# A two-layer decoder on one core: self-attention units in three pieces instead of four, later transposes, and a normalization moved to GpSimd

## The chip, the cores and the metric

The kernel runs on one core of a Trainium2 chip. The core has five engines with queues of their own: TensorE (PE; its weight loads are listed apart as PEld), VectorE (DVE), ScalarE (ACT), GpSimd (POOL) and SyncE (SP), which only issues DMAs here. Each engine takes its instructions in the order of the program and waits on semaphores. Matmul results go to PSUM, which has 8 banks of 128 x 512 float32. The metric is the device time of one execution in microseconds (us); less is better.

## The reference, cut to what matters

Two post-norm decoder layers over x (4 batches, 512 positions, 256 features), all in float32. The last layer is what the change touches:

```python
def _L1_attn_ref(x, w_qkv, w_out):           # 16 heads of 16, causal
    q, k, v = split(x @ w_qkv.T)
    scores = q @ k.T / 4 + (1 - tril) * -10000.0
    return (softmax(scores) @ v) @ w_out.T
def _L1_xattn_ref(x, ctx, ctx, mask, ...):    # 16 heads, 1601 keys
    Q, K = rope(x @ Wq.T + bq), rope(ctx @ Wk.T + bk)
    return softmax(where(mask, Q @ K.T / 4, -inf)) @ V @ Wo.T + bo
...
x = _layernorm(x + _L1_attn_ref(x, ...))
x = _layernorm(x + _L1_xattn_ref(x, ctx_1024, ctx_1024, mask, ...))
x = _layernorm(x + _L1_ffn_ref(x, ...))       # starts with a layernorm of its own
```

Before it stand the first layer's attention-like recurrence, a cross-attention and a mixture of experts, which take the first 920 us or so and are not changed.

## The kernel before, in words

The function `last_layer` (line 1278) holds the whole last layer. Its body is emitted under a manual schedule: each engine runs its instructions in the order in which the Python code emits them, and nothing is reordered. It is built twice, for `causal` true and false, and a value computed on the chip picks one; in the profile the true one ran (the affine selects of line 1599 and the score matmuls of 128, 256, 384 and 512 columns exist only there).

**Units.** The work is cut in 32 units (line 1312): first 16 of self-attention (4 batches by 4 groups of 4 heads), then 16 of cross-attention. A unit has steps, one for each key tile of 128 keys: 4 in self-attention, 13 in cross-attention. The loop over them starts after `for i, u in enumerate(units)`. A step emits:

- `scores` (1579): for each of the 4 heads a matmul of keys by queries into a bank of its own. A head uses 32 of the 128 rows of the array. In self-attention key tile k is seen only by queries from 128 k on, so the columns are 512, 384, 256 and 128.
- between the two halves (2 heads each) two calls of `next1` -> `slot1` (1509): matmuls of a *later* unit's scores, transposed, into a bank for each of two heads, whose maximum over the keys DVE takes (`most` tiles, lines 1545 and 1547). These are the softmax's maxima. They run ahead of the unit that needs them by `lead(u)` slots: 4 in self-attention, 6 in cross-attention. A self unit has 8 slots (4 query tiles by two halves), a cross unit 26.
- `exponents` (1591): ACT's Exp from each bank into an `ex` tile; in self-attention POOL's `affine_select` clears the part above the diagonal of the 128 x 128 diagonal block (both heads in one instruction).
- extra work from the unit's list `extras[i]`, spread evenly over the steps: transposes, projections for the next batch, the output projection, and so on; and one item of `quiet[i]` after each half's exponents: small work on DVE, ACT and POOL without matmuls.
- `weighted` (1612): the *previous* step's exponents times the values, 4 matmuls into one bank `po`. At the first step ACT copies it to `ot`; later DVE adds it (self), or ACT copies it to `part` and POOL adds `part` to `ot` (cross, 1637 and 1638).

All banks come from one pool of 8 (`one`).

**Around a unit.** When all slots of a unit are emitted, `negated` (1560) turns its maxima into a row of the query tile `qt` by four small DMAs. `finish` (1642) hangs the end of a unit onto the next unit's list: `divided`, and after the fourth group `turned`, `projected` (output projection, residual, statistics), then the normalization's `root` and two `apply` pairs in `quiet` (`normalize_apart`, 154). `forward` (1695) transposes the normalized x for the cross-attention queries; it is put at the head of the second unit after the batch's last one.

**The next batch.** While units (b, 0) to (b, 3) run, batch b+1 is made ready: `combined` gathers and adds expert outputs (`quiet`), `self_rows` (1385) projects keys and queries of 8 heads at a time in units 1 and 3 of the batch before; ACT copies each result to `raw`, a DMA writes it to DRAM rows (`ksd`, `qd`), and at the start of the unit after, `rows` reads it back by head into `kself` and `qt` with DMAs on SP's queue.

**The normalization.** Of `normalize_apart`: bn_stats and bn_aggr on DVE, the root on ACT (Ln, Exp: lines 132 and 134), a shift on DVE (173), and four ACT instructions of 128 x 256 (`apply`, line 178). In cross-attention it runs twice a batch: once for x (from `projected`), once more for the feed-forward's input (`block_input`, 1764), two units after the batch's last one.

Of the kernel before, what the change touches and what calls it, by code (L numbers as in the profile page):

```python
# [17 lines left out]
P = 128  # L18
# [23 lines left out]
def decoder(ctx: ExitStack, tc: tile.TileContext, a: dict, out: bass.AP):  # L42
# [111 lines left out]
    def normalize_apart(xb, into=None, rstd=rstd_ln):  # L154
# [31 lines left out]

        ends = [root, lambda: (shift(), pair(apply, 0)), lambda: pair(apply, 2)]
        return stats, [lambda t=t: pair(stats, t) for t in (0, 2)], ends
# [1089 lines left out]
    def last_layer(causal):  # L1278

        with ExitStack() as s4:  # L1280
# [220 lines left out]

            def seen(u, k):

                return k * P if causal and not u[2] else 0

            def slots1(u):
                return 2 * (1 + NT * NBIG) if u[2] else 2 * NT

            def slot1(u, s):
# [27 lines left out]
                t, c = ((i - 1) // NBIG, (i - 1) % NBIG) if cross else ((i + 2) % NT if causal else i, 0)  # L1537
                n = (t + 1) * P if causal and not cross else 512
                for j, rows, ps in tiles:
                    mm(ps[:, :n], [(qt[g][rows, t * P : (t + 1) * P], kt[rows, c * 512 : c * 512 + n])])  # L1540

                def reduce():
                    for j, rows, ps in tiles:
                        if cross:
                            nc.vector.tensor_reduce(pm[:, t, j, c : c + 1], ps, AX.X, ALU.max)  # L1545
                        else:
                            nc.vector.tensor_tensor_reduce(  # L1547
                                out=ps[:, :n],
                                in0=ps[:, :n],
                                in1=diagq[:, 384 - t * P : 384 - t * P + n],  # L1550
                                scale=1.0,
                                scalar=LOWEST,
                                op0=ALU.add,
                                op1=ALU.max,
                                accum_out=pm[:, t, j, 0:1],
                            )
# [22 lines left out]
            def scores(u, k, half, h):  # L1579
                b, g, cross = u  # L1580
                kn = kn_of(k) if cross else P
# [3 lines left out]
                q0 = seen(u, k)  # L1585
                nc.tensor.matmul(  # L1586
                    ps[:kn, q0:], kt[rows, k * P : k * P + kn], q2[rows, q0:], start=True, stop=cross or causal
                )
                return ps

            def exponents(u, k, half, pair):
                kn = kn_of(k) if u[2] else P
                ex = p4.tile([P, 2, S], F32, tag="ex", name="ex", bufs=4)
                for h, ps in enumerate(pair):
                    q0 = seen(u, k)
                    nc.scalar.activation(ex[:kn, h, q0:], ps[:kn, q0:], AF.Exp)  # L1596
                if causal and not u[2]:
                    block = ex[:, :, k * P : (k + 1) * P]
                    nc.gpsimd.affine_select(  # L1599
                        out=block, in_=block, pattern=[[0, 2], [1, P]], compare_op=ALU.is_ge,  # L1600
                        fill=0.0, base=0, channel_multiplier=-1,
                    )
                state["ex", u, k, half] = ex
# [8 lines left out]
            def weighted(u, k):  # L1612

                b, g, cross = u
                kn = kn_of(k) if cross else P
                po = one("po")
                q0 = seen(u, k)
                for j in range(4):
                    ex = state["ex", u, k, j // 2]
                    c0 = (4 * g + j) * VW  # L1620
                    nc.tensor.matmul(  # L1621
                        po[j * 32 : j * 32 + 32, q0:],
                        (vals if cross else vself)[b % 2][:kn, k, c0 : c0 + 32],
                        ex[:kn, j % 2, q0:],
                        start=True,
                        stop=True,
                    )
                last = u == units[-1]
                if k == 0:
# [9 lines left out]
                if k == (NKT if cross else NT) - 1:  # L1639
                    finish(u)  # L1640

            def finish(u):
# [39 lines left out]
                def projected(t):  # L1682
# [4 lines left out]
                    if t == 0:  # L1687
                        last = u == units[-1]
                        state["normal"] = normalize_apart(x[b], rstd=rstd_newton if last else rstd_ln)
# [23 lines left out]
                if not cross:  # L1713
                    extras[index[u] + 2].insert(0, lambda: forward(0))
                    extras[index[u] + 2].insert(1, lambda: forward(1))
# [48 lines left out]
            def block_input(b, rstd=rstd_ln):  # L1764
# [24 lines left out]
                _, pairs, ends = normalize_apart(x[b], into, rstd)  # L1789
# [78 lines left out]
            for b in range(1, B):  # L1868
# [4 lines left out]
                else:  # L1873
                    quiet[i - 2] += summed[:8]
                    quiet[i - 1] += summed[8:]
# [79 lines left out]
            for i, u in enumerate(units):  # L1955
                for f in starts[i]:
                    f()
                nk = NKT if u[2] else NT
# [13 lines left out]
                for k in range(nk):  # L1972
                    due = (u, k - 1)
                    if k == 0:
                        due = (units[i - 1], (NKT if units[i - 1][2] else NT) - 1) if i else None
                    pairs, reduces = [], []
                    for half in range(2):
                        shorter = half and causal and not u[2] and k > 1
                        if shorter:
                            reduces.append([next1()])  # L1980
                        pairs.append([scores(u, k, half, h) for h in range(2)])
                        if not shorter:
                            reduces.append([next1()])
                        if i in (14, 15) and done["n"] < ends1[units[16]] + LEADX:
                            reduces[half].append(next1())
                        if u[2]:
                            exponents(u, k, half, pairs[half])
# [4 lines left out]
                    if not u[2]:  # L1992
                        for half in range(2):
                            if not causal:
                                diagonal(k, pairs[half])
                            exponents(u, k, half, pairs[half])
# [19 lines left out]
            weighted(units[-1], NKT - 1)  # L2016

            def ending():
# [5 lines left out]
                steps, turn = block_input(B - 1, rstd_newton)  # L2024
# [163 lines left out]
```

## Time and profile before

| | us |
|---|---|
| median of 3 runs (2045.17 to 2047.63) | 2046.01 |
| the profiled execution's own time | 2047.15 |
| its span, first to last instruction | 2045.3 |
| self-attention units, first scores at 929.85 to the cross units' first scores at 1219.01 | 289.2 |
| cross-attention units, to the last weighted sum at about 1922 | 703 |

Mean granted clock of TensorE over the span: 0.983 of full speed.

How to read it: the page gives busy time by engine; a matmul's end is modelled, so a busy PE need not be at its peak. In the timeline a line is the start, the time, the engine, the line of the kernel, the operation, output <- inputs, shapes, how many were merged, and in brackets the idle time before it with what ended it. A table by stage gives for each stretch each engine's busy time, the granted clock and the DMA share.

### The profile page before, as it was taken

Reading aid. Unit: us, or ns where it says so; the run is one execution under the profiler, and the core shown is the slowest. Engines: PE = TensorE matmul, PEld = TensorE weight load, DVE = VectorE, ACT = ScalarE, POOL = GpSimd, SP = SyncE. Lnnn points to the kernel's source line nnn. Section 1 sums busy time; section 2 is a strip of 40 time slices with the busy share of each in tenths; the row PEclk is TensorE's granted clock in tenths of the full one; section 3 lists DMA queues with packets and bytes.
Section 4 is the critical chain, followed back from the end, with each engine's and each line's share of the span. In section 5 each row is a group of like instructions: output and inputs, shape, how many; then the busy total and the mean of one; then the engine's idle time right before and its main releaser. Section 6 shows DMA issues by size and latency. Waiting matters only on the chain.

```text
span 2045.3 us, 33793 instructions
## 1 busy us (share of the span) xinstructions
PE 1987.3 (97%) x12736; PEld 1228.0 (60%) x12736; DVE 1156.0 (57%) x2889; ACT 1072.4 (52%) x2244; POOL 604.0 (30%) x632
## 2 busy tenths in 40 slices
PE   9999999999999999989899999999999999999998
PEld 5768677777899999955455543333334333333366
DVE  3445334442243233356767697777777878877334
ACT  1111222224554555534556537788778788878631
POOL 3010001121222222234632324655455345333110
PEclk9999999989999999999999999999999999999999
DMA  9920411116887786743422210111210110102000
GB/s 366 356 94 1 163 65 53 53 62 258 324 313 277 269 314 259 277 131 111 124 58 59 64 60 28 55 38 47 75 45 29 58 62 18 33 17 84 1 11 33
DMA packets 80109, 242.61 MB, mean 119 GB/s; under 512 B 14134, under 2 KB 37084, under 8 KB 68028
## 3 DMA queue, kind: packets, MB, share of 16 engines
q1 hardware_dynamic: 59948, 141.45, 20.0%
q0 software_dynamic: 13152, 85.64, 11.0%
q10 hardware_dynamic: 6832, 13.20, 2.0%
q8 instruction: 105, 1.72, 0.3%
q14 instruction: 72, 0.59, 0.1%
HBM read 194.47 MB, written 56.69 MB: 123 GB/s over the span
## 4 chain that ended last, share of the span: by engine, by line
PE 49%; DVE 3%; ACT 2%; POOL 1%; DMA 1%; issue 1%; SPq 0%; ACTq 0%; POOLq 0%; DVEq 0%
PE s L1586 13%; PE one L209 12%; PE po L1621 12%; PE most L209 11%; DVE most L1547 1%; DVE pm L1545 1%; ACT x L178 1%; PE one L1652 1%; ACT ex L1596 0%; PE one L1677 0%; DMA kcd<-raw 0%; DVE st L163 0%; POOL raw L1420 0%; POOL raw L1418 0%; POOL y L1332 0%
## 5 line engine op out<-in xcount | busy, mean ns | idle before, releaser
L1596 ACT ACTIVATE ex<-s 128x512 f32<-128x512 f32 (+4 forms) x1088 | 526.7, 565 | 182.0 <-PE most L209 99.5
L1545 DVE TENSOR_REDUCE pm<-most 128x1 f32<-128x512 f32 x768 | 478.7, 683 | 101.4 <-PE most L209 99.1
L209 PE MATMUL most<-kc,qt 32*128 32x512 f32 (+1 forms) x2048 | 433.3, 540 | 1.1 <-ACT ot L1631 0.9
L1586 PE MATMUL s<-qt,kc 32*128 32x512 f32 (+1 forms) x1664 | 413.0, 622 | 1.3 <-DMA qt<-nrows 1.3
L1638 POOL TENSOR_TENSOR ot<-ot,part 128x512 f32<-128x512 f32 x180 | 228.0, 1267 | 320.2 <-ACT part L1637 320.0
L1586 PEld LDWEIGHTS s<-qt,kc 32*128 32x128 f32 (+1 forms) x1664 | 134.7, 182 | 173.2 <-ACT ex L1596 124.6
L1621 PE MATMUL po<-ex,v 128*32 128x512 f32 (+1 forms) x1664 | 227.6, 611 | 0.4 <-ACT ex L1596 0.4
L209 PEld LDWEIGHTS most<-kc,qt 32*128 32x128 f32 x2048 | 172.8, 186 | 57.8 <-issue 20.9
L1076 DVE TENSOR_TENSOR g<-g,sg 128x1024 f32<-128x1024 f32 (+1 forms) x38 | 45.5, 1198 | 215.0 <-ACT sg L1074 215.0
L1547 DVE CUSTOM_DVE_ANT_0 most<-most,c_diagq 128x384 f32<-128x384 f32 (+3 forms) x256 | 118.6, 521 | 39.0 <-PE most L209 25.8
L209 PE MATMUL wide<-xbT,eWg 128*128 128x128 f32 (+1 forms) x928 | 133.7, 304 | 1.5 <-ACT g L1074 1.5
L209 PE MATMUL wide<-xbT,eWi 128*128 128x128 f32 (+1 forms) x928 | 135.0, 306 | 0.0
L209 PEld LDWEIGHTS wide<-xbT,eWi 128*128 128x128 f32 x928 | 125.7, 192 | 8.5 <-issue 1.2
L209 PE MATMUL bank<-eWo,g 128*128 128x256 f32 x592 | 130.8, 379 | 0.0
L209 PEld LDWEIGHTS wide<-xbT,eWg 128*128 128x128 f32 x928 | 124.6, 191 | 8.3 <-ACT g L1074 1.7
L1621 PEld LDWEIGHTS po<-ex,v 128*32 128x32 f32 (+1 forms) x1664 | 34.6, 108 | 152.4 <-ACT ex L1596 147.6
L209 PEld LDWEIGHTS bank<-eWo,g 128*128 128x128 f32 x592 | 111.1, 190 | 14.3
L1637 ACT COPY part<-po 128x512 f32<-128x512 f32 x180 | 106.8, 593 | 7.5 <-PE po L1621 6.9
L1586 PE MATMUL s<-qt,ks 32*128 32x128 f32 (+3 forms) x512 | 100.5, 499 | 3.6 <-DVE at L1656 2.4
L1599 POOL TENSOR_SCALAR_AFFINE_SELECT ex<-ex 128x256 f32<-128x256 f32 x128 | 52.5, 416 | 158.0 <-ACT ex L1596 157.9
L209 PE MATMUL most<-ks,qt 32*128 32x256 f32 (+3 forms) x512 | 94.3, 488 | 3.2 <-DVE ot L1634 0.9
L698 POOL DMA_INDIRECT xs<-x,rows x32 | 31.0, 968 | 222.9 <-DVE rs L850 175.6
(333 smaller groups left out, 2910.0 us busy)
## 6 DMA issues: line engine op xcount, KB each, us to landing
xs<-zero SPq DMA_DIRECT2D x32, 512.0 KB
kc<-kcd SPq DMA_DIRECT2D x16, 800.5 KB
eWo<-in_eWo SPq DMA_DIRECT2D x8, 1408.0 KB
eWi<-in_eWi SPq DMA_DIRECT2D x8, 1028.0 KB
eWg<-in_eWg SPq DMA_DIRECT2D x8, 1028.0 KB
qt<-qd SPq DMA_DIRECT2D x32, 256.0 KB
ctxT<-in_ctxT SPq DMA_DIRECT2D x4, 1601.0 KB
kcd<-in_c_rowkc SPq DMA_DIRECT2D x4, 1601.0 KB
```

Of the source, the lines that this page charges most:

```text
L178: nc.scalar.activation(into(t), xb[:, t, :], AF.Identity, scale=mid["rs"][:, t : t + 1], bias=mid["nb"][:, t : t + 1],)
L209: nc.tensor.matmul(ps, l, r, start=(i == 0), stop=(i == n - 1))
L698: nc.gpsimd.indirect_dma_start(xs, bass.IndirectOffsetOnAxis(ap=rows[:, k * NT + t : k * NT + t + 1], axis=0), x[b][:, t, :], None)
L1076: nc.vector.tensor_tensor(part, part, dst, ALU.mult)
L1545: nc.vector.tensor_reduce(pm[:, t, j, c : c + 1], ps, AX.X, ALU.max)
L1547: nc.vector.tensor_tensor_reduce(out=ps[:, :n], in0=ps[:, :n], in1=diagq[:, 384 - t * P : 384 - t * P + n], scale=1.0, scalar=LOWEST, op0= ...
L1586: nc.tensor.matmul(ps[:kn, q0:], kt[rows, k * P : k * P + kn], q2[rows, q0:], start=True, stop=cross or causal)
L1596: nc.scalar.activation(ex[:kn, h, q0:], ps[:kn, q0:], AF.Exp)
L1599: nc.gpsimd.affine_select(out=block, in_=block, pattern=[[0, 2], [1, P]], compare_op=ALU.is_ge, fill=0.0, base=0, channel_multiplier=-1,)
L1621: nc.tensor.matmul(po[j * 32 : j * 32 + 32, q0:], (vals if cross else vself)[b % 2][:kn, k, c0 : c0 + 32], ex[:kn, j % 2, q0:], start=True ...
L1637: nc.scalar.copy(part, po)
L1638: nc.gpsimd.tensor_tensor(state["ot"], state["ot"], part, ALU.add)
```

## The change

Four edits, all in `last_layer` and in `normalize_apart`:

1. A self unit has three pieces: key tile 0; key tile 2; and key tiles 1 and 3 together. Tile 3's 128 columns lie in the free first 128 columns of tile 1's bank, so one Exp of 512 columns takes both, one affine select of 2 x 2 x 128 clears both diagonals, and `weighted` accumulates both into one `po` bank.
2. The maxima have three groups of query tiles: 2 and 0 in one bank (384 + 128 columns), 1, and 3. So a self unit has 6 slots instead of 8. `lead` stays at 4 slots. The units 14 and 15, which run ahead into the first cross unit's 26 slots, may take up to two extra slots a half instead of one.
3. `forward` is put one unit later (`index[u] + 3` instead of `+ 2`). The gathers and sums of `combined` are split 6 and 5 instead of 8 and 3 over two units.
4. In cross-attention, for all but the last batch, both normalizations apply mean and root on POOL (`aside`: a tensor_scalar with subtract and multiply, 128 x 256, scalars per partition) instead of ACT; the shift on DVE goes.

```diff
-    def normalize_apart(xb, into=None, rstd=rstd_ln):
+    def normalize_apart(xb, into=None, rstd=rstd_ln, aside=False):
...
+        def aside_apply(t):
+            nc.gpsimd.tensor_scalar(
+                into(t), xb[:, t, :], mid["mv"][:, t, 0:1], mid["rs"][:, t : t + 1], ALU.subtract, ALU.mult
+            )
+
         ends = [root, lambda: (shift(), pair(apply, 0)), lambda: pair(apply, 2)]
+        if aside:
+            ends = [root, lambda: pair(aside_apply, 0), lambda: pair(aside_apply, 2)]
...
+            def pieces(u):
+
+                if causal and not u[2]:
+                    return [(0,), (2,), (1, 3)]
+                return [(k,) for k in range(NKT if u[2] else NT)]
+
+            groups = [(2, 0), (1,), (3,)] if causal else [(t,) for t in range(NT)]
+
+            def spans(u, ks):
+
+                if len(ks) == 1:
+                    return [(ks[0], seen(u, ks[0]), seen(u, ks[0]), S)]
+                return [(k, seen(u, k), 0 if i else seen(u, k), S - seen(u, k) if i else S) for i, k in enumerate(ks)]
...
-                return 2 * (1 + NT * NBIG) if u[2] else 2 * NT
+                return 2 * (1 + NT * NBIG) if u[2] else 2 * len(groups)
...
-                t, c = ((i - 1) // NBIG, (i - 1) % NBIG) if cross else ((i + 2) % NT if causal else i, 0)
...
+                wide_, at = [], 0
+                for t in groups[i]:
+                    n = (t + 1) * P if causal else 512
+                    wide_.append((t, slice(at, at + n), n))
+                    at += n
+                for t, cols, n in wide_:
+                    for j, rows, ps in tiles:
+                        mm(ps[:, cols], [(qt[g][rows, t * P : (t + 1) * P], kt[rows, :n])])
...
-            def scores(u, k, half, h):
+            def scores(u, ks, half, h):
...
+                for k, q0, c0, c1 in spans(u, ks):
+                    kn = kn_of(k) if cross else P
+                    nc.tensor.matmul(
+                        ps[:kn, c0:c1], kt[rows, k * P : k * P + kn], q2[rows, q0:], start=True, stop=cross or causal
+                    )
...
+                c0 = min(c0 for _, _, c0, _ in spans(u, ks))
                 for h, ps in enumerate(pair):
-                    q0 = seen(u, k)
-                    nc.scalar.activation(ex[:kn, h, q0:], ps[:kn, q0:], AF.Exp)
+                    nc.scalar.activation(ex[:kn, h, c0:], ps[:kn, c0:], AF.Exp)
...
+                for i, (k, q0, e0, e1) in enumerate(parts):
+                    kn = kn_of(k) if cross else P
+                    for j in range(4):
+                        ex = state["ex", u, ks, j // 2]
+                        c0 = (4 * g + j) * VW
+                        nc.tensor.matmul(
+                            po[j * 32 : j * 32 + 32, q0:],
+                            (vals if cross else vself)[b % 2][:kn, k, c0 : c0 + 32],
+                            ex[:kn, j % 2, e0:e1],
+                            start=i == 0,
+                            stop=i == len(parts) - 1,
+                        )
...
-                        state["normal"] = normalize_apart(x[b], rstd=rstd_newton if last else rstd_ln)
+                        state["normal"] = normalize_apart(
+                            x[b], rstd=rstd_newton if last else rstd_ln, aside=cross and not last
+                        )
...
-                    extras[index[u] + 2].insert(0, lambda: forward(0))
-                    extras[index[u] + 2].insert(1, lambda: forward(1))
+                    extras[index[u] + 3].insert(0, lambda: forward(0))
+                    extras[index[u] + 3].insert(1, lambda: forward(1))
...
-            def block_input(b, rstd=rstd_ln):
+            def block_input(b, rstd=rstd_ln, aside=True):
...
-                _, pairs, ends = normalize_apart(x[b], into, rstd)
+                _, pairs, ends = normalize_apart(x[b], into, rstd, aside)
...
-                    quiet[i - 2] += summed[:8]
-                    quiet[i - 1] += summed[8:]
+                    quiet[i - 2] += summed[:6]
+                    quiet[i - 1] += summed[6:]
...
-                for k in range(nk):
-                    due = (u, k - 1)
+                for k, ks in enumerate(cut):
+                    due = (u, cut[k - 1])
...
-                        shorter = half and causal and not u[2] and k > 1
+                        shorter = half and causal and not u[2] and ks == (2,)
...
-                        if i in (14, 15) and done["n"] < ends1[units[16]] + LEADX:
-                            reduces[half].append(next1())
+                        for _ in range(2 if causal else 1):
+                            if i in (14, 15) and done["n"] < ends1[units[16]] + LEADX:
+                                reduces[half].append(next1())
```

## The prediction

> **What bounds the kernel now.** I read the page first: TensorE is busy 97% of the span, so a gain must come from its own time, its gaps or its clock.
>
> ```profile
> PE 1987.3 (97%) x12736; PEld 1228.0 (60%) x12736; DVE 1156.0 (57%) x2889; ACT 1072.4 (52%) x2244; POOL 604.0 (30%) x632
> ```
>
> Next the table by stage: a batch turn in self-attention, its end, and a cross stage. Columns: window, length, busy time of PE, PEld, DVE, ACT, POOL, granted clock, DMA share, GB/s.
>
> ```profile
> 1028.00:1092.00 64.00, 59.57 (x468) 33.70 (x467) 45.99 (x185) 37.52 (x94) 23.44 (x41) 0.97 0.24 67
> 1157.00:1219.00 62.00, 58.35 (x434) 31.13 (x429) 51.92 (x139) 24.20 (x60) 15.73 (x28) 0.92 0.14 42
> 1400.00:1580.00 180.00, 179.05 (x1376) 67.23 (x1368) 138.93 (x258) 143.46 (x280) 95.48 (x77) 1.00 0.17 55
> ```
>
> Self-attention leaves PE idle for 4 us in 64 and loses clock. Cross-attention has PE full, ACT at 80%, DVE at 77% and POOL at 53%. PE's waits from 960 to 1164 (total, times, longest):
>
> ```profile
> PE one L1698 <- ACT x L178: 5.1, 12, 1.2
> PE one L209 <- ACT ex L1596: 2.5, 8, 0.5
> PE s L1586 <- DVE at L1656: 2.4, 2, 1.3
> ```
>
> The timeline of a self turn shows the first wait, and how late the next batch's queries come:
>
> ```profile
> 1018.36 0.93 PE L209 MATMUL most<-ks,qt 32*128 32x384 f32 x8 [0.87 <-ACT ot L1631]
> ...
> 1029.87 2.07 ACT L178 ACTIVATE x<-x,nb,rstd 128x256 f32<-128x256 f32 x4 [0.23 <-DVE nb L173]
> 1030.52 0.33 PE L1698 MATMUL one<-ident,x 128*128 128x128 f32 x1 [1.20 <-ACT x L178]
> ...
> 1043.95 1.98 PE L209 MATMUL one<-xT,qkvQ 128*128 128x512 f32 x4
> 1046.59 0.61 SPq L1307 DMA_DIRECT2D qd<-raw  x1
> 1051.08 0.33 SPq L1310 DMA_DIRECT2D qt<-qd  x1
> 1053.91 0.59 PE L209 MATMUL most<-ks,qt 32*128 32x384 f32 x2
> ```
>
> The query projection ends at 1045.9; its result goes through DRAM into `qt`, and the first maxima of the unit start at 1053.9, 8.0 us on (1010.2 to 1018.36 a turn earlier). In a cross turn ACT's normalization stands between exponentials:
>
> ```profile
> 1453.87 1.08 ACT L178 ACTIVATE x<-x,nb,rstd 128x256 f32<-128x256 f32 x2
> 1455.32 1.10 ACT L178 ACTIVATE x<-x,nb,rstd 128x256 f32<-128x256 f32 x2
> 1456.31 2.03 ACT L1596 ACTIVATE ex<-s 128x512 f32<-128x512 f32 x4
> 1456.95 1.98 PE L209 MATMUL one<-xT,xaQ 128*128 128x512 f32 x4 [0.35 <-ACT ex L1596]
> ```
>
> **The change part by part.** Minus is a gain; all of it against the profiled execution, 2047.15 us (span 2045.3 and 1.85 around it), 1.1 above the median. The 920 us ahead stay.
>
> *Three pieces.* In a self step scores and maxima run side by side in different rows. Before, each step has 640 columns a head (512+128, 384+256, ...) and takes 1.36 us without `po`: 5.44 a unit. With two maxima groups of lead, the pieces have 512+512, 256+512 and 512+256. For 1024 columns a base cross step has 2.95 less `po` 1.06 = 1.89; 768 lies between, some 1.55. So 5.0 a unit. `po` has the same columns in one group fewer, some 0.1. 16 units by 0.55: **-9**. Bounds: 0, where DVE keeps the pace (52 of 62 us in the last self stage; its work of a unit doesn't shrink), and -12. Exp instructions go from 16 to 12 a unit; ACT at 24 to 38 us in these stages isn't the bound. The affine select of four blocks (0.41 us for two) is hidden behind the next piece.
>
> *Transposes later.* The wait on `x` (5.1 us over three turns) ends, and the half clock that follows it, about 2, 2 and 3.6 us in 1032-1036, 1096-1101 and 1162-1169, has less cause: -13.6 at most. Late next: a unit further on, key projections and transposes come together, and the projection waits for ACT's copies of `xT` behind exponentials, some 1.6 at each of three turns: +5. Net **-9**, bounds -13 and 0.
>
> *Gathers split 6 and 5.* DVE reaches the sums behind `at` earlier in one unit and later in the other: **-2**, and the lighter steps around give -2 more; bounds +3 and -5. SP and POOL issue the same DMAs.
>
> *The lead.* It stays at 4 slots, but that is now two thirds of a unit. The first maxima of the unit after next stood at the third of four steps; now they are at the second of three. What they need, queries through DRAM, took 8.0 us from the projection's end and was just in time. From the new order of PE's instructions, with the durations above, PE stands there after 3.9 us at the first turn's unit 4, 5.2 at units 6 and 10, about 7 at units 8 and 12, and some 3 short for the first cross unit. Waits: 4.2 + 2x2.9 + 2x1 + 3 = 15, of which 0.9 is paid already. Behind the waiting matmul stand PE's scores, and behind these the Exps and DVE's maxima: nothing covers it. If three of these waits draw a half-clock stretch at 2 each, +6: **+20**. Bounds: +5, if issue and landing (0.6 and 4.47 + 3.30 us on the chain) come faster where SP's queue is empty, and +42, if all six places cost wait plus clock and the longest doubles.
>
> *Projection in the next unit.* `projected` shares a lighter step with copies of `at` behind a 512-column Exp: 1.8 + 1.8 + 0.9 = **+4**; bounds 0 and 6. Units 14 to 16, with up to two extra maxima a half, stay at DVE's pace: 0, bounds -2 and +4.
>
> Self together: -9 -9 -4 +20 +4 = **about +2**.
>
> *GpSimd normalizes.* 24 ACT instructions of 0.54 us leave ACT: 13 us, plus six shifts on DVE. What it is worth is read off steps of PE (start of one `po` to the next): where the same step costs 4.84 elsewhere, the turn at 1451.6 took 7.26; all excess over such steps is 5.4, 7.9 and 6.5 at the three turns, 19.8 in sum. ACT's wait for `mv` (0.56) and the root (0.5) stay, six times, so I take **-14**; bounds -18.5 and 0. POOL's price is bounded by its own rows of tensor-scalar:
>
> ```profile
> L1638 POOL TENSOR_TENSOR ot<-ot,part 128x512 f32<-128x512 f32 x180 | 228.0, 1267 | 320.2 <-ACT part L1637 320.0
> L1784 POOL TENSOR_SCALAR x<-x 128x1024 f32<-128x1024 f32 x4 | 11.1, 2768 | 54.3 <-ACT ln L178 54.3
> L1762 POOL TENSOR_SCALAR bob<-bob 128x256 f32<-128x256 f32 x1 | 0.9, 869 | 4.7 <-DMA cx<-in_ctxT 4.7
> ```
>
> A pair is 2 x 0.87 = 1.74 against 1.08 on ACT. Queued behind it on POOL: the sums of `part` (1.27 each, one a step) and the rotation of keys (3 x 1.27). A projection step of 4.84 holds pair, sum and 1.27 of rotation, 4.3; with two pairs close together POOL falls behind by about 2 us and `part`, in two buffers, absorbs one step. At 1.5 us an apply, ACT would wait for `part`, and the 14 would be gone. The self batch's turn inside the first cross units stays on ACT; only its transposes move: -1.
>
> The Trainium skill ("GPSIMD Engine Reference", section "4.1 Engine selection") sends elementwise work to VectorE and so speaks against the move. By the rows DVE has the spare time only in principle (77% busy, with the 0.7 us maxima between), POOL is at 53%; the move loses only if POOL gets onto the path.
>
> **Sum.** +2 -14 -1 = about -12: 2047.15 - 12 = **2035**.
>
> On the clock the windows of a cross turn show something:
>
> ```profile
> 1646.00:1648.00 2.00, 1.57 (x6) 0.47 (x10) 0.76 (x2) 2.00 (x5) 0.00 (x0) 0.77 0.00 0
> 1648.00:1650.00 2.00, 2.00 (x12) 0.34 (x12) 0.62 (x1) 1.43 (x4) 0.00 (x0) 0.50 0.00 0
> ```
>
> One wait of 0.43 us in two stands before a stretch at 0.50. So the 3 to 4 us waits at `qt` may well draw one each; that is the +6 above. "TensorE: Matmul & The Clock Gate", section "What's actually happening", halves the clock only after an idle window of about 3.4 us. By that page only the 4.2 us wait would, and the sum would be some 4 lower, an estimate of about 2031; the row decides, as it shows a half clock with far less idle time.
>
> **The rivals.** A difference under 0.2%, 4.1 us, can't be told from none here.
>
> *Self gains too.* SP's queue is emptier than I take it, the waits at `qt` cost 5 to 8 and not 20: self -18 and +6, cross -15, about **2020**. For it: issue of `qt` at 1051.08 waits on the DMA before it, not on the queue; against it: the same 8.0 us at both turns, with different neighbours.
>
> *POOL hands the gain back.* ACT's copy of `part` waits for POOL's sum, which waits behind two pairs; cross gives 0 to -6, self +2: **2046**. For it: POOL has a backlog at projections already (rotations end to end); against it: 47% of POOL is free in the stage and a step's need fits.
>
> *Slower: the round trip of the queries.* Place: the first maxima of units 4, 6, 8, 10, 12 and the first cross unit, in the second piece of the unit two before. Price: 8.0 us less what PE has to do till then, plus about 2 us of half clock at each: 15 + 12, and up to 42 if ACT's `raw` copy and DMA issue slip too. The other self edits give 18 (9 + 9 + 4 - 4) and cross 15: it is even at 33 and decides from 37. At 42: **2056**. For it: DRAM transfers can't be shortened by lighter steps; against it: part of the wait can be filled by PE's queued weights and the previous half's scores.
>
> **How the numbers follow.** Likeliest case (cross gain, self about level) 0.55: 2035, its own range 2026 to 2042. Self gains too 0.12: 2020. POOL hands it back 0.11: 2046. Slower 0.22: 2056. The range: below, half of the second case (from 2023); above, the slow case's own price, 2056. Faster 0.67, same 0.10, slower 0.23.
>
> **What would show it.** Self units (first scores at 929.85 to cross's first at 1219.01) should take about 291 us, not 289.2; PE's waits on `x` L178 gone; new waits of `most` on DMA `qt` in six places, 1 to 4 us each. In cross, no ACT applies at the three turns, the step of 7.26 near 5.3, POOL's applies about 0.87 us. I am wrong if waits at `qt` stay under 1 us (then 2020), if they exceed 6 (then slower), or if POOL's applies take 1.5.

## The result, and the profile after

The changed kernel is a little slower: 2050.33 us median against 2042.84 for the kernel before in the same comparison, a ratio of 1.0035 (95% interval 1.0025 to 1.0046). The forecast was 2035 and faster. The rival that happened is the slow one, the round trip of the queries. The changed kernel's profiled execution took 2052.24 us (span 2050.5), against 2047.15 (2045.3).

| profiled executions, us | before | after | difference | forecast |
|---|---|---|---|---|
| self-attention, first scores to the cross units' first scores | 289.2 | 309.8 | +20.6 | +2 |
| from the cross units' first scores to the end | 826.3 | 813.3 | -13.0 | -15 |
| start of the self units | 929.85 | 927.44 | -2.4 | 0 |

The page of the changed kernel: TensorE is busy 1977 us instead of 1987, in a span that is 5 us longer.

```profile
PE 1977.1 (96%) x12736; PEld 1229.8 (60%) x12736; DVE 1156.1 (56%) x2867; ACT 1054.1 (51%) x2156; POOL 627.3 (31%) x624
```

The table by stage of the changed kernel (the columns as before). The first window is the one shown of before; the second is the end of self-attention, which now lies later; the third is the cross stage.

```profile
1028.00:1092.00 64.00, 53.59 (x418) 31.10 (x411) 40.70 (x156) 31.82 (x72) 19.91 (x30) 0.89 0.22 64
1184.00:1237.00 53.00, 52.32 (x399) 29.99 (x398) 47.85 (x114) 19.79 (x42) 14.11 (x21) 0.94 0.16 49
1400.00:1580.00 180.00, 179.65 (x1424) 68.77 (x1422) 139.06 (x262) 141.40 (x276) 107.88 (x89) 1.00 0.17 55
```

In the first window PE now stands for 10.4 us instead of 4.4, at a clock of 0.89 instead of 0.97. All engines do less there, so something else is late. The waits of PE from 920 to 1230 (total, times, longest) name it:

```profile
PE most L216 <- DMA qt<-qd: 19.1, 4, 9.1
PE one L216 <- DMA cx<-in_ctxT: 4.6, 2, 3.1
PE s L1619 <- DVE at L1695: 2.1, 1, 2.1
```

The 5.1 us of waits on the normalized `x` are gone, as forecast. 19.1 us on the queries have come, and 4.6 on chunks of the context, for which the prediction had no term. PE's timeline has the places:

```profile
944.87 2.11 PE L216 MATMUL most<-ks,qt 32*128 32x384 f32 x16 [9.09 <-DMA qt<-qd]
...
1034.57 2.11 PE L216 MATMUL most<-ks,qt 32*128 32x384 f32 x16 [4.29 <-DMA qt<-qd]
...
1072.64 2.10 PE L216 MATMUL most<-ks,qt 32*128 32x384 f32 x16 [2.89 <-DMA qt<-qd]
```

A fourth stands at 1139.82 (2.87 us). Each is the second piece of a unit, at the first maxima of the unit two further on: units 0, 4, 6 and 10 wait for the queries of units 2, 6, 8 and 12. The chain of waits of the changed kernel shows the way of unit 6's queries, from ACT's copy to the matmul:

```profile
1026.16 0.61 ACT raw L1399
...
1026.78 5.09 DMA qd<-raw
...
1031.94 2.54 DMA qt<-qd
...
1034.57 1.59 PE most L216 x5
```

The largest wait, in unit 0, has a second cause beside the lead. SP's queue in unit 0 of the changed kernel (start, time, DMA):

```profile
927.71 4.87 SPq L1314 DMA_DIRECT2D kcd<-raw  x2
932.63 0.45 SPq L2012 DMA_DIRECT2D c_cos<-in_c_cos  x1
933.13 0.42 SPq L2012 DMA_DIRECT2D c_sin<-in_c_sin  x1
935.10 2.32 SPq L1608 DMA_DIRECT2D qt<-nrows  x4
937.53 2.36 SPq L1314 DMA_DIRECT2D kcd<-raw  x2
941.46 0.33 SPq L1317 DMA_DIRECT2D ks<-ksd  x1
941.84 0.43 SPq L1317 DMA_DIRECT2D qt<-qd  x1
```

In the kernel before, the reads of `ks` and `qt` were issued from 934.60 on, ahead of the tables `c_cos` and `c_sin`; four writes of context keys (`kcd`) stood in front of them there too. And PE needed these queries later:

```profile
928.80 5.70 SPq L1307 DMA_DIRECT2D kcd<-raw  x4
934.60 0.42 SPq L1310 DMA_DIRECT2D ks<-ksd  x1
935.07 0.42 SPq L1310 DMA_DIRECT2D qt<-qd  x1
...
936.96 0.43 SPq L1970 DMA_DIRECT2D c_sin<-in_c_sin  x1
...
940.57 0.59 PE L209 MATMUL most<-ks,qt 32*128 32x384 f32 x2
```

Before, the first maxima of unit 2 came 10.7 us after the first scores of unit 0, without a wait. In the changed kernel PE was ready for them at 935.78, 8.3 us after, which is the lead at work; and now the reads stand behind the tables. The reason is in the code: ahead of unit 0 a loop emits maxima until the lead is reached, two slots at a time, and takes one item of the unit's list with each turn. With 8 slots a unit it ran 6 turns and the sixth item was the read; with 6 slots it runs 5. The chain puts the landing of `c_sin` right before the read:

```profile
933.13 8.31 DMA c_sin<-in_c_sin
941.84 2.90 DMA qt<-qd
```

(The semaphore numbers in the trace show that the DMAs use eight semaphores in turns: the read of `ks` at 941.46 uses the one of `c_sin` again and is issued when `c_sin` has landed, and the read of `qt` stands behind it.)

The clock comes on top. Windows of 4 us around the wait in unit 6:

```profile
1068.00:1072.00 4.00, 1.75 (x22) 0.72 (x20) 1.88 (x7) 2.01 (x5) 3.26 (x4) 1.00 0.58 188
1072.00:1076.00 4.00, 3.36 (x21) 2.25 (x22) 1.13 (x5) 0.36 (x2) 3.67 (x4) 0.52 0.65 226
1076.00:1080.00 4.00, 4.00 (x16) 2.78 (x19) 3.83 (x16) 1.01 (x4) 0.45 (x2) 0.63 0.00 0
```

By these shares PE runs at half clock from about 1072.2 to 1079.0, some 7 us, and the stretch begins about 0.5 us before the wait of 2.89 us ends. The longest stretch lies in unit 0. It begins ahead of the wait of 9.09 us (935.78 to 944.87) and lasts to 949.3, 20.5 us in all:

```profile
929.00:937.00 8.00, 6.78 (x20) 3.39 (x18) 5.16 (x22) 2.91 (x7) 5.76 (x12) 0.50 0.55 148
937.00:945.00 8.00, 0.13 (x4) 0.16 (x4) 0.00 (x0) 0.00 (x0) 0.00 (x0) 0.50 0.70 242
945.00:949.00 4.00, 4.00 (x23) 2.69 (x24) 1.98 (x12) 0.00 (x0) 0.00 (x0) 0.50 0.19 59
```

Summed over windows of 1 us (one less the clock, from 920 to 1960) the half clock stands for 30.7 us after and 22.2 before. All of the 30.7 and 13.6 of the 22.2 lie in self-attention, 17.1 more; the forecast had 6 for the stretches behind the waits.

### The profile page after: what moved, and what is told of

Same layout as the page of the kernel before. It is cut to its first block, busy times and chain, and to the rows that moved or that the text cites. A ratio compares the mean times of both kernels' runs of the same rounds, so it can differ in the third digit from the quotient of the medians.

```text
span 2050.5 us, 33586 instructions
## 1 busy us (share of the span) xinstructions
PE 1977.1 (96%) x12736; PEld 1229.8 (60%) x12736; DVE 1156.1 (56%) x2867; ACT 1054.1 (51%) x2156; POOL 627.3 (31%) x624
## 4 chain that ended last, share of the span: by engine, by line
PE 47%; DVE 4%; DMA 2%; ACT 2%; POOL 1%; issue 1%; SPq 0%; DVEq 0%; POOLq 0%; ACTq 0%
PE one L216 12%; PE s L1619 12%; PE po L1659 11%; PE most L216 10%; DVE pm L1565 1%; DVE most L1580 1%; PE one L1691 1%; DMA qd<-raw 1%; ACT ex L1629 1%; DMA qt<-qd 1%; POOL x L188 1%; ACT x L178 1%; DMA cx<-in_ctxT 0%; DMA c_sin<-in_c_sin 0%; PE one L1716 0%
## 5 line engine op out<-in xcount | busy, mean ns | idle before, releaser
L1629 ACT ACTIVATE ex<-s 128x512 f32<-128x512 f32 (+2 forms) x1024 | 519.1, 589 | 162.7 <-PE most L216 104.0
L216 PE MATMUL most<-kc,qt 32*128 32x512 f32 (+1 forms) x2048 | 422.6, 531 | 0.7 <-ACT ex L1629 0.4
L1619 PE MATMUL s<-qt,kc 32*128 32x512 f32 (+1 forms) x1664 | 407.2, 616 | 0.0
L216 PE MATMUL most<-ks,qt 32*128 32x128 f32 (+3 forms) x512 | 84.4, 506 | 19.5 <-DMA qt<-qd 19.1
L1636 POOL TENSOR_SCALAR_AFFINE_SELECT ex<-ex 128x256 f32<-128x256 f32 (+1 forms) x96 | 46.5, 487 | 179.5 <-ACT ex L1629 179.2
```

The costliest lines, as they stand in the source:

```text
L216: nc.tensor.matmul(ps, l, r, start=(i == 0), stop=(i == n - 1))
L1619: nc.tensor.matmul(ps[:kn, c0:c1], kt[rows, k * P : k * P + kn], q2[rows, q0:], start=True, stop=cross or causal)
L1629: nc.scalar.activation(ex[:kn, h, c0:], ps[:kn, c0:], AF.Exp)
L1636: nc.gpsimd.affine_select(out=block, in_=block, pattern=pattern, compare_op=ALU.is_ge, fill=0.0, base=0, channel_multiplier=-1,)
```

## The experiments

Ratios are to the kernel before, run in the same comparison; self-attention is that of the profiled execution, measured as in the table above.

**Reads ahead of the tables.** One more item of unit 0's list is run before the tables are loaded.

```diff
                 if i == 0:
+                    work.pop(0)()
                     for t, name in ((cosT, "c_cos"), (sinT, "c_sin")):
```

> The changed kernel, with one more item of the first unit's list run ahead of the loads of c_cos and c_sin, so that SP's queue has the second half's keys and queries before the tables, as the kernel before has it; the rest is the changed kernel. Theory (queue order): the 9.1 us wait of the first unit's maxima on qt goes, that unit falls from 27.7 us to about 17, and the whole time by 9 to 12 us, to about 2040 (ratio to the kernel before about 0.999). Rival (three pieces are slower by themselves, DVE sets the pace and the wait only hides it): the first unit stays above 23 us and the time falls by less than 4. The waits in the fifth, seventh and eleventh unit (4.3, 2.9, 2.9) stay in both.

Measured: ratio 1.0000 (0.9986 to 1.0014), 2044.58 us, some 7 less than the changed kernel by the ratios: between theory and rival. Unit 0 takes 22.25 us instead of 27.68, and a wait of 6.93 is left of 9.09. So the order of the tables is about half of what unit 0 loses (it takes 17.38 in the next run), neither the whole of it nor nothing. SP's queue of this run shows what is still in front:

```profile
928.89 6.76 SPq L1314 DMA_DIRECT2D kcd<-raw  x4
935.75 0.41 SPq L1317 DMA_DIRECT2D ks<-ksd  x1
936.20 0.42 SPq L1317 DMA_DIRECT2D qt<-qd  x1
```

Four writes of rotated context keys, which wait for GpSimd's rotation. The kernel before had the same four in front; its reads went out 4.8 us after its first scores, here 7.1. But it needed the queries 10.7 us after, here 5.0 (933.67, against first scores at 928.63), so most of the wait that is left comes from needing them sooner.

**Reads ahead of the waiting writes too.** The writes of unit 0 are held back until the reads are issued.

```diff
-                        flush(1)
+                        flush(state.get("hold", 1))
...
-                k1_, q1_, *keys0[2:4], lambda: (keys0[6](), keys0[7]()), lambda: (flush(0), rows1()),
+                lambda: (state.update(hold=5), k1_()), q1_, *keys0[2:4],
+                lambda: (keys0[6](), keys0[7]()),
+                lambda: (rows1(), flush(0), state.update(hold=1)),
...
+                    work.pop(0)()
```

> The changed kernel with the second half's first keys and queries read ahead of the tables and also ahead of the four writes of context keys (kcd), which wait for GpSimd's rotation; the writes follow the reads. Running the reads ahead of the tables alone left a wait of 6.9 us in the first unit, with 6.8 us of kcd writes in front on SP's queue. Theory (SP's queue in order: reads stand behind writes that wait for GpSimd): the wait falls under 1.5 us, the first unit to 17 us or less and the whole time by 5 to 9 more than the tables' order alone gave, to about 2037 (ratio 0.996 to 0.998). Rival (the reads are late for their own reason: the projection, its copy on ACT, its way through DRAM): the wait stays over 5 and the time within 3 us of the run with the tables' order alone.

Measured: 0.9975 (0.9961 to 0.9990), 2042.09 us. The wait in unit 0 is gone, and the unit takes 17.38 us. So with the shorter lead too the reads come in time if nothing stands in front of them. The whole gained 5 us over the run before it by the ratios, at the lower end of what was expected; the self-attention of the profiled execution stayed at 303.7 (304.0 in the run before it), as it lost more to the clock later on (34.1 us by the same sum over the whole, 25.6 in the run before it).

**Projections earlier.** The key and query projections of the next batch come one or two steps earlier in their units (1, 3, 5 and 9); the order in unit 0 is that of the changed kernel.

```diff
-                    into.insert(min(1, len(into)), divided)
+                    into.insert(min(1 if cross or g or b == B - 1 else 2, len(into)), divided)
...
-                extras[i + 2] = keys1[n : n + 3] + extras[i + 2]
+                extras[i + 2] = extras[i + 2] + keys1[n : n + 3] if i else keys1[n : n + 3] + extras[i + 2]
```

> The changed kernel, with the next batch's key and query projections one or two steps earlier in their unit (ahead of the transposes of ot in units 1, 5 and 9, ahead of the context keys in unit 3); the tables stay in front of the second half's queries. Theory (round trip of the queries, 8 us, covered too little): the waits of maxima on qt in units 4, 6 and 10 (4.3, 2.9, 2.9 us, 10 in sum) fall under 1 us each and the time by 8 to 14 us with the half clock behind them, to about 2039; the 9.1 us in unit 0 stays. Rival (the maxima only wait in DVE's place; DVE is then late): the same waits come back on pm or s, and the time falls by under 4.

Measured: 0.9974 (0.9960 to 0.9989), 2040.72 us, 0.6% less than the changed kernel (12 us, by the difference of the ratios). The waits in units 6 and 10 are gone. The one in unit 0, which this run leaves alone, was 12.1 here. The one in unit 4 is still 3.76, and SP's queue of this run has again writes ahead of it:

```profile
1013.51 0.62 SPq L1314 DMA_DIRECT2D ksd<-raw  x1
1014.23 0.61 SPq L1314 DMA_DIRECT2D qd<-raw  x1
1014.95 9.64 SPq L1314 DMA_DIRECT2D kcd<-raw  x3
1024.69 0.40 SPq L1317 DMA_DIRECT2D ks<-ksd  x1
1025.18 0.51 SPq L1317 DMA_DIRECT2D qt<-qd  x1
```

The queries were written at 1014; their read was issued 11 us later, behind three writes of context keys.

**All three mends.** The edits of the two runs above together, and in unit 4 the reads before the writes of unit 3:

```diff
+                    if b == 1 and c == 1:
+                        extras[i + 3][0] = lambda f=extras[i + 3][0]: (state.update(hold=5), f())
+                        starts[i + 4].append(lambda: (flush(0), state.update(hold=1)))
```

> The changed kernel with all mends of the queries' way: reads ahead of tables and of waiting kcd writes in unit 0, projections earlier in units 1, 3, 5 and 9, and in unit 4 the reads ahead of the kcd writes of unit 3. Theory: no wait of maxima on qt above 1.5 us anywhere; self-attention about 284 us instead of 310 and of 289 before; whole time about 2025, ratio 0.990 to 0.993, so that three pieces do pay. Rival (DVE sets the pace of the new units): self-attention stays at 292 or more, the waits come back on pm and at, whole time above 2033.

Measured: 0.9915 (0.9892 to 0.9937), 2026.55 us; self-attention 281.5. In a later comparison the same kernel gave 0.9905 (0.9889 to 0.9921) and 280.6.

> The three-piece kernel with all mends once more, beside the four-step kernel on the same chip: 0.991 of the kernel before, as in its first run, by every theory; self-attention 281 to 284 us.

PE's waits from 920 to 1225 in the first of these runs, the two largest groups:

```profile
PE one L216 <- DMA cx<-in_ctxT: 4.4, 2, 3.0
PE s L1619 <- DVE at L1695: 3.3, 2, 1.8
```

No wait on the reads of `qt` is left. DVE does not take its place (3.3 us of waits on its `at`, 2.1 in the changed kernel): the rival that DVE sets the pace falls. The waits on context chunks stay. The half clock is down to 10.2 us. This kernel beats both, by 0.9% the one before and by 1.2% the changed one. So 28 us of self-attention in the profiled executions (309.8 to 281.5), some 24 by the ratios of the whole time, hung on the order of a few DMAs and projections.

**A smaller lead.** The lead of the maxima in self-attention is 2 slots instead of 4; nothing else is mended.

```diff
-                return LEADX if u[2] else 4
+                return LEADX if u[2] else 2
```

> The changed kernel with a lead of 2 slots instead of 4 in self-attention, nothing else mended. Theory: first maxima come a piece, some 5 us, later, so the waits on qt of 4.3, 2.9 and 2.9 us go and the first unit's 9.1 falls to about 4; against it the maxima's rows (nrows, four small DMAs) get one piece less, about 5 us instead of 10, and scores of each next unit wait on them up to 2 us at some of 15 units. I expect 0 to 12 us less than the changed kernel, about 2044. Rival (the lead isn't what makes the queries late): no less than the changed kernel, waits on qt as they were.

Measured: 0.9943 (0.9922 to 0.9964), 2034.48 us, some 19 us less than the changed kernel by the ratios, more than the 0 to 12 expected. Self-attention is 292.0. Its waits of PE from 920 to 1225:

```profile
PE most L216 <- DMA qt<-qd: 6.3, 2, 3.1
...
PE s L1619 <- DMA qt<-nrows: 3.4, 2, 2.4
```

The waits on `qt<-qd` stand in unit 0 (3.13 us, though the tables are in front of the reads) and at the first cross unit's maxima (3.14; the changed kernel has none there). Those in units 4, 6 and 10 are gone with this one constant. So it was the lead, kept at 4 slots while a unit shrank to 6, that made the queries late there, and it has about 6 of the 9 us in unit 0. The price, waits on `nrows`, is 3.4 us.

**GpSimd's part undone.**

```diff
-                            x[b], rstd=rstd_newton if last else rstd_ln, aside=cross and not last
+                            x[b], rstd=rstd_newton if last else rstd_ln, aside=False
...
-            def block_input(b, rstd=rstd_ln, aside=True):
+            def block_input(b, rstd=rstd_ln, aside=False):
```

> The changed kernel with the cross-attention normalizations back on ACT (part 4 undone). Theory: cross-attention and what follows take 13 us more, 826 instead of 813 from the first cross scores on; whole time about 2063, ratio about 1.010. Rival (the 13 us come from how the self units end and not from GpSimd): under 4 us more, ratio under 1.006.

Measured: 1.0067 (1.0048 to 1.0086), 2059.19 us. That is 0.3% or 6.5 us above the changed kernel; from the first cross scores on the profiled execution took 819.7 us, 6.4 more than 813.3. Half of the 13 expected, between theory and rival.

**GpSimd's part alone**, on the kernel before (the hunks of the change on `normalize_apart`, `aside` and `block_input`).

> The kernel before with part 4 alone: both cross-attention normalizations applied on GpSimd, self units as before. Theory: self-attention 289 us as before, cross-attention and the rest 813 instead of 826: ratio 0.9935 to 0.995, some 2030 against 2043. Rival (part 4 pays only behind the changed self units): within 4 us of the kernel before.

Measured: 0.9948 (0.9932 to 0.9964), 2036.10 us, some 10.6 less by the ratio. The part pays by itself. In the profiled execution 820.1 us lie behind the first cross scores, 6.2 less than before, with 8.5 us lost to half clock in cross-attention, as much as in the profile of before: a comparison at equal clock.

What the part is worth at one turn is seen in PE's timeline, at the second of the three turns in cross-attention (start of one weighted sum to the next is a step). With ACT's normalization, in the changed kernel with the part undone:

```profile
1643.19 1.06 PE L1659 MATMUL po<-ex,v 128*32 128x512 f32 x8
1650.45 1.06 PE L1659 MATMUL po<-ex,v 65*32 65x512 f32 x8
1653.38 1.06 PE L1659 MATMUL po<-ex,v 128*32 128x512 f32 x8
1658.85 1.07 PE L1659 MATMUL po<-ex,v 128*32 128x512 f32 x8
```

and with GpSimd's, in the changed kernel:

```profile
1645.52 1.07 PE L1659 MATMUL po<-ex,v 128*32 128x512 f32 x8
1651.38 1.06 PE L1659 MATMUL po<-ex,v 65*32 65x512 f32 x8
1654.31 1.06 PE L1659 MATMUL po<-ex,v 128*32 128x512 f32 x8
1658.79 1.07 PE L1659 MATMUL po<-ex,v 128*32 128x512 f32 x8
```

The two long steps go from 7.26 to 5.86 and from 5.47 to 4.48: 2.4 us for this turn, not the 4.7 that 14 over three turns makes. The kernel before had, at this same turn, 7.26, then 5.79, then 5.59 where the run with the part undone has 3.4: PE was at half clock there, as at two other places of its cross-attention (8.5 us in all by the sum over windows). The run with the part undone has none of these stretches though ACT normalizes in it, and neither has the changed kernel. So half clock wasn't the price of ACT's normalization, and of the 13.0 us that the profiles of before and after differ by, 6.4 are GpSimd's and about half is clock that comes and goes. It does so with the same code too: the run with the writes held back, equal to the changed kernel in cross-attention, lost 3.4 us near 1820, the changed kernel nothing.

**Transposes back.** All three mends, with `forward` two units after the batch.

```diff
-                    extras[index[u] + 3].insert(0, lambda: forward(0))
-                    extras[index[u] + 3].insert(1, lambda: forward(1))
+                    extras[index[u] + 2].insert(0, lambda: forward(0))
+                    extras[index[u] + 2].insert(1, lambda: forward(1))
```

> The run with all mends, with the transposes of the normalized x back at two units after the batch (part 3 undone). Theory of the prediction: PE waits on x at three turns again, 5 us, and 3 to 6 us of half clock follow: 6 to 13 us more than with all mends, about 2034. Rival (the later place costs as much at its new neighbours): within 3 us of the run with all mends.

Measured: 0.9952 (0.9936 to 0.9968), 2036.83 us; self-attention 291.4 instead of 281.5. So the later transposes are worth 9.9 us in the three-piece kernel's self-attention, 7.6 by the ratios of the whole time. The waits on `x` were shorter than before the change (1.0 us in sum), but two waits on `qt` (4.3 us in sum) came back, in units 6 and 10. The transposes push the projections back: the queries were written 0.1 us after the start of unit 6 (1046.4 and 1046.3), with all mends 3.3 us ahead of it (1038.8 and 1042.1).

**Four steps, with the other parts.** The kernel before with parts 3 and 4.

> The kernel before with part 3 (transposes of the normalized x a unit later, gathers 6 and 5) and part 4 (GpSimd normalizes in cross-attention), but with the four steps a unit, eight slots of maxima and lead of before. It tells what the three pieces are worth where the queries are in time. With all mends the three-piece kernel took 281.5 us in self-attention and 2026.6 in all. Theory of the prediction (a piece fewer is worth 9 us, the later transposes 9): self-attention about 281 + 9 = 290 less what PE's waits on x gave, some 284 to 288, whole time 2029 to 2034. Rival (the pieces are worth nothing by themselves, and the transposes and GpSimd are all of it): self-attention 279 to 282 and the whole time within 3 us of the mended three-piece kernel.

Measured: 1.0004 (0.9994 to 1.0014), 2055.07 us beside 2053.96 for the kernel before in that comparison; self-attention 300.8. Both theories missed: four steps with the later transposes are slower in self-attention than before (289.2), where a gain was expected. PE's timeline in unit 6:

```profile
1072.50 1.09 PE L1593 MATMUL s<-qt,ks 32*128 32x256 f32 x4 [4.03 <-DVE at L1663]
```

Unit 6 took 20.8 us, 15.4 in the kernel before. By the code, the later transposes now meet the values' projections and DVE's sums of the next batch in one unit.

**Gathers split as before.** The same four-step kernel, and the three-piece kernel with all mends, with the gathers split 8 and 3:

```diff
-                    quiet[i - 2] += summed[:6]
-                    quiet[i - 1] += summed[6:]
+                    quiet[i - 2] += summed[:8]
+                    quiet[i - 1] += summed[8:]
```

> The four-step kernel with later transposes and GpSimd's normalizations, but the gathers and sums split 8 and 3 over two units as before. The four-step kernel with the split 6 and 5 took 300.8 us in self-attention against 289.2 before, with a wait of 4.0 us on DVE's at in unit 6. Theory (the split: sums that fall into the second unit stand in front of DVE's at): that wait goes, self-attention 282 to 290, whole time 0.990 to 0.996 of the kernel before. Rival (the transposes a unit later do it, in the unit that also projects the values): self-attention stays at 297 or more, whole time within 0.2% of before.

> The three-piece kernel with all mends, with the gathers split 8 and 3 as before. Theory (three pieces have six quiet places a unit, so eight items spill to the unit's end): 1 to 6 us more in self-attention than 281, whole time 0.991 to 0.995 of the kernel before. Rival (the split matters to neither): within 1 us in self-attention.

Measured with four steps: 0.9990 (0.9975 to 1.0004), 2041.89 us; self-attention 295.0, 5.8 less than with 6 and 5, but still 4.5 above the four-step kernel with GpSimd's part alone (290.5), from which only the place of the transposes now sets it apart. Unit 6 alone takes 19.9 us in it, 15.4 with the transposes at their old place. The wait on `at` went to 3.2 only. So the later place costs something there, and the theory that the split alone does it falls; its rival had 297 or more, which was missed too. What the split costs with four steps isn't sure: the two whole times lie 0.14% apart, with intervals that overlap. With three pieces: 0.9933 (0.9912 to 0.9954), 2029.39 us; self-attention 281.0, within 0.5 of the mended kernel: the split matters little there, as the rival said.

## Why the prediction was wrong

**The step that failed** is the term "The lead", taken at +20. The late queries cost 28.3 us of self-attention (309.8 less 281.5 with the mends), inside the bounds of +5 and +42 given for the step. The mechanism was right: queries through DRAM that were just in time, and a lead that became two thirds of a unit. Three of the waits came as worked out: with PE standing in units 4, 6 and 10, 4.2 and twice 2.9 us were forecast, and 4.29, 2.89 and 2.87 measured. (These are the units in which PE stands. The list of places under the slow rival gives such numbers to the units whose queries are late; those were 6, 8 and 12.) The 1 us each in units 8 and 12 and the 3 us ahead of the first cross unit did not come.

What the step put at nothing is unit 0, where PE waited 9.09 us for unit 2's queries. Two things meet there. One is the same lead: with a lead of 2 slots 3.13 were left. The other is the order on SP's queue: the loop ahead of unit 0 takes one item fewer, and the reads fall behind two tables. With the tables behind the reads again 6.93 were left, and none with the four waiting writes behind them as well. The prediction asked of that queue whether it would be fuller or emptier, not in which order it would stand. So the waits on `qt` summed to 19.1 us instead of 15, and the half clock to 17.1 us more instead of 6.

**The other terms of the sum** failed too, by as much. Self-attention was forecast at +2 and came at +20.6, 18.6 off: 8.3 of it is the lead (28.3 for 20), and 10.3 is the rest, -9 -9 -4 +4 = -18 forecast against -7.7 with the queries in time (289.2 to 281.5). Part of this is known: 4.4 us of waits on chunks of the context, which the mended kernel still has and the prediction didn't count, and the terms below.

With gains of 7.7 in self-attention and 13.0 in cross-attention the slow rival was even at 20.7, not at 33. Its 2056 came from a price of 42 against 33, measured were 28.3 against 20.7. That the differences are near, 9 and 7.6, is luck. (The 7.6 is the table's +20.6 - 13.0 once more; the profiled executions differ by 5.1, as the self units start 2.4 us earlier, and the medians by 7.5.) Two sums of the prediction are also off by about 1 us: +2 -14 -1 is -13, and 5.1 with 2, 2 and 3.6 us makes 12.7, not 13.6.

**The half clock.** The prediction weighed the Trainium skill here ("TensorE: Matmul & The Clock Gate", section "What's actually happening"). The stretches of the changed kernel's self-attention lasted 3.4 or 6.8 us, the one in unit 0 20.5, all multiples of 3.4, which agrees with the window length of that page. What doesn't agree is the condition of a whole idle window: the stretch in unit 6 began when PE had stood for about 2.4 of its 2.89 us, and with all mends one of 3.4 us still followed a wait of 1.78 us (1054.71). What sets these off no run here isolates.

**The transposes and the pieces**, forecast at -9 each, depend on each other. Self-attention in four arrangements, with GpSimd's part in all of them, and with all mends in the three-piece ones:

| | transposes two units on | three units on |
|---|---|---|
| four steps | 290.5 | 295.0 |
| three pieces | 291.4 | 281.0 (281.5 and 280.6 with the gathers split 6 and 5) |

(The 291.4 has the gathers split 6 and 5, the other three 8 and 3, and with it 4.3 us of waits on `qt` came back.) By itself neither gains here; together they gain some 9 us, half of the 18 that the prediction had added up. Why the three pieces bear the later transposes and four steps do not is not shown beyond the place of the loss, unit 6.

**GpSimd's normalization**, forecast at -14, gave 6.4 in profiled executions without half clock in cross-attention, 6.2 in two with the same 8.5 us of it, and 6.5 and 10.6 (each with some 3 to 5 either way) by the ratios. The sign and the place were right; the size was about half. Of the excess of 19.8 us over steps elsewhere (5.4, 7.9 and 6.5), the second and third turns held half clock that ACT's normalization did not cause. And GpSimd's rows show 1.22 us for each apply, not the 0.87 taken from the nearest row (one with a constant for its scalar); the other twelve applies, into `ln`, have the same mean:

```profile
L188 POOL TENSOR_SCALAR x<-x,mv,rstd 128x256 f32<-128x256 f32 x12 | 14.6, 1224 | 6.9 <-DVE pm L1565 6.9
```

It lies between 0.87 and the 1.5 at which the gain was to be gone. The long step came to 5.86 where 5.3 was forecast; that the slower apply is the reason is likely but not shown. The Trainium skill ("GPSIMD Engine Reference", section "4.1 Engine selection") would put such work on VectorE, which no run here tries. Against ACT GpSimd is the slower one, 1.22 us for an apply that took 0.54; the kernel gains all the same, since GpSimd has the time (108 of 180 us busy in the cross stage) and ACT stood in PE's way.

**The other rivals.** "Self gains too" is in kind what the mended kernel does, with -7.7 in self-attention and not -12; the changed kernel does not. "POOL hands the gain back" had 0 to -6 for cross-attention, near the 6.2 to 6.4 that the part is worth, but not by its mechanism: in the changed kernel's cross-attention ACT's copies of `part` never wait for POOL. POOL does come onto the path at one place, the third turn, behind two pairs of applies (the wait is 0.2 with the part undone):

```profile
1822.20 0.66 PE L1691 MATMUL one<-ident,ot 128*128 128x128 f32 x4 [0.94 <-POOL ot L1677]
```

## What to carry to other kernels

When a loop that hands out side work gets fewer turns, every item behind it moves, also past DMAs that are not part of the change: compare the order on the DMA queue itself and look for reads that fall behind large loads or behind writes that wait for another engine. A lead that is counted in slots changes in time when the slots are repacked; give it again in microseconds, against the measured way of the data that it needs. Edits of one pipeline don't add: price them in the arrangement in which they will stand, and when an excess is read off a trace, take out the stretches of half clock first.

## What the runs showed of the hardware

A GpSimd tensor-scalar with two scalars per partition took 1.22 us for 128 x 256 float32; the one with a constant took 0.87. Around waits of TensorE under 3 us stood stretches of 3.4 or 6.8 us at half clock, and the number of such stretches in cross-attention differed between executions of kernels that are alike there: 8.5 us in the profiled execution of before, none in that of the changed kernel with ACT's normalization put back. The load of the table `c_sin` took 8.31 us from issue to landing, and a small read that used its semaphore next was issued only then.
